# Selective-scan kernel: scan inputs of every second state from TensorE, y sums with h as the moving operand

## The chip, the cores and the metric

The kernel runs on one core of a Trainium2 chip. The metric is the device time of one execution in microseconds (us), taken as the median of several runs. TensorE (PE in the profile), VectorE (DVE), ScalarE (ACT), GpSimd (POOL) and SyncE (SP) each work through their own list of instructions in order and wait for one another through semaphores.

## The reference

The input x has 16 sequences of 256 steps and 256 features, with one conditioning vector each. Four layers follow one another: a low-rank adapter made from the conditioning vector (L0), a two-way selective state-space layer with a gated MLP (L1), a transformer block with 16 heads of 64 (L2) and one with 16 heads of 16 (L3). The part that the change touches is the state-space layer; for each sequence it is done once forwards and once backwards in time:

```python
xs, z = split(h @ in_w);  xs = silu(xs)                 # 512 inner channels each
proj = xs @ xproj_w
dt = softplus(proj[..., :512] + dt_bias)
Bm, Cm = proj[..., 512:576], proj[..., 576:640]         # 64 states
A = -exp(A_log)                                          # 512 x 64
def step(hst, ins):                                      # over the 256 time steps
    dA = exp(dt_t[:, :, None] * A)
    hst = hst * dA + (dt_t * x_t)[:, :, None] * B_t[:, None, :]
    y_t = einsum('bds,bs->bd', hst, C_t)
y = ys + xs * Dskip
return y * silu(z) @ out_w
```

Everything is in float32.

## The kernel before

**Units and states.** A unit is one sequence in one direction: 32 units, done one after the other. For each unit the kernel loops over the 64 states, so there are 2048 steps k = (u, s). In a step one state of all 512 channels is handled over all 256 times: 4 chunks (IC) of 128 channels on the partitions, each with 256 times along the free dimension, hence tiles h of 128 x 1024.

**One step.** `drive` (four steps ahead, AHEAD = 4) lets POOL write the scan's input h = dtx * B, where B of one state is a row that a DMA has spread over all partitions (`load_b`, tiles bb, four states a load) (L931). `decay` lets ACT write exp(dt * A) for the state into PSUM, in two tiles of 2 x 256 taken from a ring of three (L946, four instructions a state); column 0 of each chunk stays 0, so that a scan can run over two chunks and begin afresh at the second. `scan` lets DVE run two scans of 512 in place in h (L974); for the backward direction they run over the tile from its end. Then h is multiplied with C: in five of eight states by DVE with a C row that TensorE has spread into PSUM (`spread`, tile cs, L961, product L977), in three of eight by POOL with a C row that a DMA has spread (`load_c`, tile cb, product L981). `add_up` (two steps behind, BEHIND = 2) sums over the states in PSUM: eight transposes of 128 x 128 blocks of h add into y (L992), h being the stationary operand and the identity the moving one.

```python
nc.tensor.matmul(
    ys[u][:, t, c * P : (c + 1) * P], h[:, c, t * P : (t + 1) * P], ident, ...
    is_transpose=True, ...
```

**Beside the loop.** The loop over k is written out in Python; between its steps it advances two generators. `pend` does `back` of the unit before (the product with out_w) and `front` of the unit to come (projections pxz and pdt at L393 and L423, softplus, dt and dtx; load_front's weights). `other` does `rest(b)`, all of L1's MLP, L2 and L3 of a finished sequence (products dense, down, sc, pt, po, scT at L500 to L711), one or two pieces a step. After a unit's last state y is turned back (yt on ACT, py on TensorE, L1165 and L1172) and multiplied with silu(z). The scheduler may shift neighbouring instructions of an engine; POOL's products are kept in program order.

**Buffers.** h tiles come from a ring of NH = 11. PSUM has eight banks: two for y, three for the decays, one for cs, and two (ps_g) that all other products share. The last sequence's `rest` runs alone at the end and then also uses the decay and cs banks.

Of the kernel before, what the change touches and what calls it, by code (L numbers as in the profile page):

```python
# [15 lines left out]
P = 128  # L16
# [6 lines left out]
NS = 64  # L23
EPS = 1e-5


# [28 lines left out]
def kernel(ctx: ExitStack, tc: tile.TileContext, a: dict, out: bass.AP):  # L55
# [68 lines left out]
    SG = 4  # L124
    ND = 3
    NH = 11
    res = ctx.enter_context(tc.tile_pool(name="res", bufs=1))
# [6 lines left out]
    ps_y = ctx.enter_context(tc.tile_pool(name="ps_y", bufs=1, space=PSUM))  # L134
    ps_c = ctx.enter_context(tc.tile_pool(name="ps_c", bufs=1, space=PSUM))
    ps_g = ctx.enter_context(tc.tile_pool(name="ps_g", bufs=2, space=PSUM))
# [119 lines left out]
    for d in ("fwd", "bwd"):  # L256
        an = res.tile([P, IC, NS], F32, name=f"a_neg_{d}")
        nc.sync.dma_start(an, a[f"L1_cond_{d}_A_log"].rearrange("(c p) s -> p c s", p=P))
        nc.scalar.activation(an, an, AF.Exp)
        nc.vector.tensor_scalar(an, an, -1.0, None, ALU.mult)  # L260
        a_neg.append(an)
        w_bc.append(res.tile([P, IC, 2 * NS], F32, name=f"w_bc_{d}"))
        nc.sync.dma_start(w_bc[-1], chunked(a[f"L1_cond_{d}_xproj_w"])[:, :, DI:])
        w_out.append(res.tile([P, IC, D], F32, name=f"w_out_{d}"))
        nc.sync.dma_start(w_out[-1], chunked(a[f"L1_cond_{d}_out_w"]))


    decays = [ps_y.tile([P, 2, T], F32, name=f"decay{j}") for j in range(ND)]
    for dc in decays:
        nc.vector.memset(dc[:, :, 0:1], 0.0)  # L270

# [101 lines left out]
    def front(u):  # L373
# [15 lines left out]
        for m in range(0, 2 * IC, 2):  # L389
            px = halves(bank1("pxz"))  # L390
            for j in range(2):
                for c in range(DC):
                    nc.tensor.matmul(  # L393
                        px[:, j], w_in[:, c, (m + j) * P : (m + j + 1) * P], hT[:, c],
                        start=(c == 0), stop=(c == DC - 1),
                    )
                yield
            nc.scalar.copy(xz[:, m : m + 2], px)
        nc.scalar.activation(xz, xz, AF.Silu)
# [9 lines left out]
        yield  # L409
        pt = bank1("pct")  # L410
        for t in range(NT):
            nc.tensor.transpose(pt[:, t * P : (t + 1) * P], bc[:, t * P : (t + 1) * P], ident)
        cT = s2.tile([P, NT, NS], F32, name="cT")
        nc.scalar.copy(cT, pt[:, :T].rearrange("p (t s) -> p t s", t=NT)[:, :, NS:])
        yield


# [43 lines left out]
        tc.keep_in_program_order(nc.gpsimd.tensor_tensor(dtx, dt, xz[:, 0:IC], ALU.mult))  # L461
        st[u] = (xz, cT, bd, dt, dtx)
        yield

    def back(u, yg):
# [12 lines left out]
        for m in range(DC):  # L478
            xb = xs[b][:, m]
            nc.vector.scalar_tensor_tensor(  # L480
                xb, po[:, m], m_mamba[:, 4 + m, b : b + 1], xb, ALU.mult, ALU.add
            )
# [409 lines left out]

    bbs, cbs, ys, made, hs, skips = {}, {}, {}, {}, {}, {}
    cs = ps_c.tile([P, 2, T], F32, name="cs")
    steps = [(u, s) for u in range(len(units)) for s in range(NS)]
    turn = [0]

    def load_b(u, g):
        bd = st[u][2]
        bb = s3.tile([P, SG, T], F32, name="bb")  # L900
        nc.sync.dma_start(bb, bd[g * SG : (g + 1) * SG, :].partition_broadcast(P))
        bbs[u, g] = bb

    def load_c(u, g):
        bd = st[u][2]
        cb = s3.tile([P, 3, T], F32, name="cb")
        nc.sync.dma_start(
            cb,
            bd[NS + 8 * g + 1 : NS + 8 * g + 8 : 3, :].partition_broadcast(P),
        )  # L910
        cbs[u, g] = cb

    def drive(k):
        u, s = steps[k]
        if s % SG == 0:
            if s == 0:
                load_b(u, 0)
            if s + SG < NS:
                load_b(u, s // SG + 1)
            if s % 8 == 0:  # L920
                load_c(u, s // 8)
        if s == 0:
# [4 lines left out]
            skips[u] = skip  # L927
        h = s3.tile([P, IC, T], F32, name="h", bufs=NH)
        bb = bbs[u, s // SG][:, s % SG]
        tc.keep_in_program_order(  # L930
            nc.gpsimd.tensor_tensor(h, st[u][4], bb.unsqueeze(1).to_broadcast([P, IC, T]), ALU.mult)  # L931
        )
        hs[k] = h

    def decay(k):
        u, s = steps[k]
        d = units[u][1]

        when = slice(1, T) if d == 0 else slice(T - 2, None, -1)
        made[k] = []  # L940
        for i in range(2):
            dc = decays[turn[0] % ND]
            turn[0] += 1
            for j in range(2):
                c = 2 * i + (j if d == 0 else 1 - j)
                nc.scalar.activation(  # L946
                    dc[:, j, 1:T], st[u][3][:, c, when], AF.Exp, scale=a_neg[d][:, c, s : s + 1]
                )
            made[k].append(dc)


    near = [k for k, (u, s) in enumerate(steps) if s % 8 in (0, 2, 3, 5, 6)]
    nth = {k: i for i, k in enumerate(near)}

    def spread(i):

        if i >= len(near):
            return
        u, s = steps[near[i]]
        for t in range(NT):  # L960
            nc.tensor.transpose(  # L961
                cs[:, i % 2, t * P : (t + 1) * P], st[u][1][:, t, s : s + 1].to_broadcast([P, P]), ident
            )

    def scan(k):
        u, s = steps[k]
        d = units[u][1]
        h = hs[k]
        for i, dc in enumerate(made.pop(k)):
            hv = h[:, 2 * i : 2 * i + 2].rearrange("p c t -> p (c t)")  # L970
            dv = dc.rearrange("p c t -> p (c t)")
            if d == 1:
                hv = hv[:, ::-1]
            nc.vector.tensor_tensor_scan(hv, dv, hv, 0.0, ALU.mult, ALU.add)  # L974
        if k in nth:
            c = cs[:, nth[k] % 2]
            nc.vector.tensor_tensor(h, h, c.unsqueeze(1).to_broadcast([P, IC, T]), ALU.mult)  # L977
        else:
            c = cbs[u, s // 8][:, (s % 8) // 3]
            tc.keep_in_program_order(  # L980
                nc.gpsimd.tensor_tensor(h, h, c.unsqueeze(1).to_broadcast([P, IC, T]), ALU.mult)  # L981
            )

    def add_up(k):
        u, s = steps[k]
        if s == 0:
            ys[u] = ps_y.tile([P, NT, DI], F32, name="y")

        for n, h in enumerate(([skips.pop(u)] if s == 0 else []) + [hs.pop(k)]):
            for t in range(NT):  # L990
                for c in range(IC):
                    nc.tensor.matmul(  # L992
                        ys[u][:, t, c * P : (c + 1) * P], h[:, c, t * P : (t + 1) * P], ident,
                        start=(s == 0 and n == 0 and c == 0),
                        stop=(s == NS - 1 and c == IC - 1), is_transpose=True,
                        skip_group_check=True,
                    )

# [140 lines left out]
    for k in range(AHEAD):  # L1139
        drive(k)  # L1140
    decay(0)
    spread(0)
    spread(1)
    other = late()
    for k in range(len(steps) + BEHIND):
        if k < len(steps):
# [6 lines left out]
            if k + 1 < len(steps):  # L1153
                decay(k + 1)
        if k >= BEHIND:
            add_up(k - BEHIND)
        if k - 1 in nth:
            spread(nth[k - 1] + 2)
        if k >= BEHIND:
            u, s = steps[k - BEHIND]  # L1160
            if s == NS - 1:
                b, d = units[u]
                yt = s1.tile([P, NT, DI], F32, name="yt", tag="uu")
                for t in range(NT):
                    nc.scalar.copy(yt[:, t], ys[u][:, t])  # L1165
                yg = s1.tile([P, IC, T], F32, name="yg", tag="pr")
                for i in range(2):
                    py = halves(bank1("py"))
                    for j in range(2):
                        c = 2 * i + j  # L1170
                        for t in range(NT):
                            nc.tensor.transpose(py[:, j, t * P : (t + 1) * P], yt[:, t, c * P : (c + 1) * P], ident)  # L1172
                    nc.vector.tensor_tensor(
                        yg[:, 2 * i : 2 * i + 2], py, st[u][0][:, IC + 2 * i : IC + 2 * i + 2], ALU.mult
                    )
                pend = beside((u, yg), u + 2)
# [5 lines left out]
    drain(other)  # L1182
    alone += [None] + [t.rearrange("p c t -> p (c t)") for t in (decays[0], cs, decays[1])]
    alone += [None, decays[2].rearrange("p c t -> p (c t)")]
    while waiting:
# [29 lines left out]
```

## Time and profile before

| | |
|---|---|
| median of 3 runs | 7622.63 us (7620.03 to 7626.16) |
| span of the profiled execution, first to last instruction | 7616.3 us |
| median less span | 6.3 us |
| mean granted TensorE clock | 0.932 |
| first scan, last scan (start) | 139.5 us, 7383.1 us |
| DMA share of the 16 engines, q1 | 26.7%, 669.44 MB |
| sum of TensorE's waits on y for POOL's C product (L981) | 639.1 us |
| sum of ACT's waits on decay for DVE's scan | 1289.9 us |

The page gives no time of its own for the profiled execution beside its span; the median of the runs stands for what lies around it. In a group's line of the profile the columns are: line, engine, operation, out<-in by the program's names, shapes, how often (x), then busy time in us, mean ns of one, and the idle time of the engine just before the group with what ended most of it. PEld is the loading of TensorE's stationary operand. Matmul records overlap, so that their mean length is not their rate.

### The profile page before, as it was taken

The numbers are of one execution on the slowest core, as the hardware profiler recorded it, in microseconds if no ns is written. First come the engines' busy times: TensorE is split into PE (matmuls) and PEld (weight loads), VectorE is DVE, ScalarE is ACT, GpSimd is POOL, SyncE is SP. The second block draws the span as 40 slices with busy tenths as digits, with TensorE's granted clock in tenths as the row PEclk, the third lists the DMA queues.
The fourth block names the chain that finished last, engine by engine and source line by source line (L and its number), as shares of the span: only waits on it lengthen the run. The fifth ranks groups of instructions, "written<-read, shape, count | busy, mean of one in ns | idle before, by whom it ended". The sixth has DMA issues, their size and how long they took to land.

```text
span 7616.3 us, 100847 instructions
## 1 busy us (share of the span) xinstructions
PE 6249.2 (82%) x35471; PEld 4952.4 (65%) x35471; DVE 6860.6 (90%) x6887; ACT 5431.2 (71%) x12141; POOL 6843.8 (90%) x2959
## 2 busy tenths in 40 slices
PE   7568888888888888888888888888888888888778
PEld 4456676666667666676666666666666766666655
DVE  3988999999999999999999999999999999999982
ACT  4567777777777777777777777777777777777753
POOL 3999999999999999999999999999999999999960
PEclk8679999999999999999999999999999999999999
DMA  4112232222322222232222223222232222322221
GB/s 166 54 65 92 89 102 76 87 92 88 103 85 93 80 91 95 92 103 73 88 92 91 100 86 98 78 92 93 87 106 79 94 84 89 101 91 89 73 68 49
DMA packets 331644, 675.90 MB, mean 89 GB/s; under 512 B 24724, under 2 KB 204032, under 8 KB 326784
## 3 DMA queue, kind: packets, MB, share of 16 engines
q1 hardware_dynamic: 331136, 669.44, 26.7%
q8 instruction: 280, 4.59, 0.2%
q14 instruction: 228, 1.87, 0.1%
HBM read 650.22 MB, written 10.75 MB: 87 GB/s over the span
## 4 chain that ended last, share of the span: by engine, by line
DVE 47%; POOL 15%; issue 14%; ACT 12%; PE 10%; DVEq 0%; POOLq 0%; ACTq 0%
DVE h L974 34%; POOL h L931 8%; DVE h L977 8%; ACT decay L946 5%; POOL h L981 5%; PE y L992 3%; DVE maxima L682 1%; ACT L155 1%; PE dense L500 1%; PE down L511 1%; PE bank L108 1%; PE po L605 1%; POOL uu L452 1%; POOL dt L458 1%; POOL dtx L461 1%
## 5 line engine op out<-in xcount | busy, mean ns | idle before, releaser
L974 DVE TENSOR_TENSOR_SCAN h<-decay,h 128x512 f32<-128x512 f32 x4096 | 4748.8, 1213 | 283.1 <-ACT decay L946 196.6
L931 POOL TENSOR_TENSOR h<-dtx,bb 128x1024 f32<-128x1024 f32 x2048 | 4793.5, 2367 | 129.2 <-PE y L992 128.4
L992 PE MATMUL y<-ident,h 128*128 128x128 f32 x16384 | 2385.3, 292 | 693.0 <-POOL h L981 639.1
L992 PEld LDWEIGHTS y<-ident,h 128*128 128x128 f32 x16384 | 2054.6, 151 | 1047.6 <-POOL h L981 733.1
L946 ACT ACTIVATE decay<-dt,a_neg_bwd 128x255 f32<-128x255 f32 x4096 | 1816.8, 471 | 759.9 <-DVE h L974 718.3
L946 ACT ACTIVATE decay<-dt,a_neg_fwd 128x255 f32<-128x255 f32 x4096 | 1824.6, 474 | 613.0 <-DVE h L974 571.6
L981 POOL TENSOR_TENSOR h<-h,cb 128x1024 f32<-128x1024 f32 x768 | 1813.2, 2361 | 289.8 <-DVE h L974 275.1
L977 DVE TENSOR_TENSOR h<-h,cs 128x1024 f32<-128x1024 f32 x1280 | 1533.5, 1215 | 66.2 <-PE cs L961 56.6
L961 PE MATMUL cs<-ident,cT 128*128 128x128 f32 x2560 | 521.6, 294 | 131.8 <-DVE h L977 130.3
L961 PEld LDWEIGHTS cs<-ident,cT 128*128 128x128 f32 x2560 | 331.4, 147 | 216.0 <-DVE h L977 192.0
L572 PE MATMUL sc<-k,q 64*128 64x256 f32 x960 | 293.4, 429 | 16.7 <-ACT ex L581 16.0
L393 PE MATMUL pxz<-hTm,w_in 128*128 128x256 f32 x1024 | 267.6, 388 | 15.9 <-DVE maxima L682 12.1
L679 PE MATMUL sc<-kd,qk 128*128 128x512 f32 x490 | 251.4, 614 | 33.5 <-DVE maxima L682 20.8
L700 PE MATMUL scT<-qk,kd 128*128 128x256 f32 x984 | 251.1, 386 | 28.7 <-DVE qk L691 23.2
L581 ACT ACTIVATE ex<-sc,nmax 128x256 f32<-128x256 f32 x480 | 222.7, 468 | 71.2 <-DVE nmax L577 68.5
L423 PE MATMUL pdt<-xz,w_dt 128*128 128x256 f32 x1024 | 247.3, 385 | 0.0
L572 PEld LDWEIGHTS sc<-k,q 64*128 64x128 f32 x960 | 172.6, 200 | 105.3 <-issue 34.2
L393 PEld LDWEIGHTS pxz<-hTm,w_in 128*128 128x128 f32 x1024 | 181.4, 194 | 53.1 <-DVE maxima L682 15.5
L700 PEld LDWEIGHTS scT<-qk,kd 128*128 128x128 f32 x984 | 175.5, 190 | 60.7 <-ACT pr L429 25.0
L577 DVE TENSOR_REDUCE nmax<-sc 128x2 f32<-128x512 f32 x240 | 163.9, 683 | 49.5 <-PE sc L572 48.8
L423 PEld LDWEIGHTS pdt<-xz,w_dt 128*128 128x128 f32 x1024 | 190.7, 194 | 22.2
L595 ACT COPY exT<-pt 128x512 f32<-128x512 f32 x240 | 140.0, 583 | 86.2 <-PE pt L591 84.0
(350 smaller groups left out, 7571.4 us busy)
## 6 DMA issues: line engine op xcount, KB each, us to landing
bb<-bd SPq DMA_DIRECT2D x512, 512.0 KB
cb<-bd SPq DMA_DIRECT2D x256, 384.0 KB
l2w<-in_L_cond_W_dram SPq DMA_DIRECT2D x32, 1024.0 KB
l3w<-in_L_cond_W_dram SPq DMA_DIRECT2D x32, 1024.0 KB
l1w<-in_L_cond_mlp_w_dram SPq DMA_DIRECT2D x48, 512.0 KB
w_in<-in_L_cond_fwd_in_w_dram SPq DMA_DIRECT2D x16, 1024.0 KB
w_dt<-_L_cond_fwd_xproj_w_dram SPq DMA_DIRECT2D x16, 1024.0 KB
w_in<-in_L_cond_bwd_in_w_dram SPq DMA_DIRECT2D x16, 1024.0 KB
```

The lines of the kernel that those rows point to most:

```text
L393: nc.tensor.matmul(px[:, j], w_in[:, c, (m + j) * P : (m + j + 1) * P], hT[:, c], start=(c == 0), stop=(c == DC - 1),)
L423: nc.tensor.matmul(pp[:, j], w_dt[:, c, (m + j) * P : (m + j + 1) * P], xz[:, c], start=(c == 0), stop=(c == IC - 1),)
L572: nc.tensor.matmul(sc[:, t], q[base : base + 64, ch, t * P : (t + 1) * P], k[base : base + 64, ch], start=True, stop=True,)
L679: nc.tensor.matmul(sc, q[:, g, t * P : (t + 1) * P], kd[g % 2][:, 2 * i : 2 * i + 2], start=True, stop=True)
L700: nc.tensor.matmul(sc[:, kt], kd[g % 2][:, j, kt * P : (kt + 1) * P], q[:, g], start=True, stop=True)
L931: nc.gpsimd.tensor_tensor(h, st[u][4], bb.unsqueeze(1).to_broadcast([P, IC, T]), ALU.mult)
L946: nc.scalar.activation(dc[:, j, 1:T], st[u][3][:, c, when], AF.Exp, scale=a_neg[d][:, c, s : s + 1])
L961: nc.tensor.transpose(cs[:, i % 2, t * P : (t + 1) * P], st[u][1][:, t, s : s + 1].to_broadcast([P, P]), ident)
L974: nc.vector.tensor_tensor_scan(hv, dv, hv, 0.0, ALU.mult, ALU.add)
L977: nc.vector.tensor_tensor(h, h, c.unsqueeze(1).to_broadcast([P, IC, T]), ALU.mult)
L981: nc.gpsimd.tensor_tensor(h, h, c.unsqueeze(1).to_broadcast([P, IC, T]), ALU.mult)
L992: nc.tensor.matmul(ys[u][:, t, c * P : (c + 1) * P], h[:, c, t * P : (t + 1) * P], ident, start=(s == 0 and n == 0 and c == 0), stop=(s == ...
```

## The change

Every second state (odd s) gets its scan input from TensorE and its decays in SBUF; even states keep POOL's input and have their decays in PSUM.

- `diagonals`: for each group of four states POOL multiplies the identity with two columns of B, which gives diagonal matrices dg (128 x 512 an instruction); bT is B turned on TensorE in `front`, where C was turned before.
- `turn`: once a unit, dtx is transposed into xT (8 transposes, 2 ACT copies).
- `put_in`: for an odd state, 8 products xT x dg write the scan's input into PSUM, slot 1. One step later DVE scans it there.
- `decay`: an even state's decays go to PSUM slot 0, an odd state's into an h tile. Column 0 of dt is set to 1e34 (APART) and a_neg is kept at or below -1e-30 (LEAST), so that exp gives 0 there; one scan of 1024 then covers all four chunks.
- C: all rows by DMA (four states a load); even states are multiplied on POOL, odd ones on DVE.
- `add_up`: two products of 512 columns a state with the identity as the stationary and h as the moving operand, without transposing.
- Backward units have time turned round once, when xz is copied, and once when the result is added to x; scans always run forwards.
- y no longer has to be turned back (yt and py go). NH is 9. PSUM: y two banks, slots 0 and 1 two each, ps_g two.

```diff
-    ND = 3
-    NH = 11
+    NH = 9
...
-        nc.vector.tensor_scalar(an, an, -1.0, None, ALU.mult)
+        nc.vector.tensor_scalar(an, an, -1.0, LEAST, ALU.mult, ALU.min)
...
-    decays = [ps_y.tile([P, 2, T], F32, name=f"decay{j}") for j in range(ND)]
+    slots = [ps_y.tile([P, IC, T], F32, name=f"slot{j}") for j in range(2)]
...
-            nc.scalar.copy(xz[:, m : m + 2], px)
+            nc.scalar.copy(xz[:, m : m + 2], px[:, :, ::-1] if d else px)
...
+        tc.keep_in_program_order(nc.gpsimd.memset(dt[:, :, 0:1], APART))
...
+    def diagonals(u, g):
+        dg = s3.tile([P, NT, SG // 2, P], F32, name="dg")
+        tc.keep_in_program_order(
+            nc.gpsimd.tensor_tensor(
+                dg,
+                ident.unsqueeze(1).unsqueeze(1).to_broadcast([P, NT, SG // 2, P]),
+                st[u][4][:, :, g * SG + 1 : (g + 1) * SG : 2].unsqueeze(3).to_broadcast([P, NT, SG // 2, P]),
+                ALU.mult,
+            )
+        )
...
+    def turn(u):
+        xT = s1.tile([P, NT, DI], F32, name="xT")
+        for t in range(NT):
+            pt = bank1("pxt")
+            for c in range(IC):
+                nc.tensor.transpose(pt[:, c * P : (c + 1) * P], st[u][3][:, c, t * P : (t + 1) * P], ident)
+            nc.scalar.copy(xT[:, t], pt)
...
     def decay(k):
+        if s % 2:
+            dc = hs[k] = s3.tile([P, IC, T], F32, name="h", bufs=NH)
+        else:
+            dc = slots[0]
+        for c in range(IC):
+            nc.scalar.activation(dc[:, c], st[u][2][:, c], AF.Exp, scale=a_neg[d][:, c, s : s + 1])
+
+    def put_in(k):
+        u, s = steps[k]
+        dg = dgs[u, s // SG]
+        for t in range(NT):
+            for c in range(IC):
+                nc.tensor.matmul(
+                    slots[1][:, c, t * P : (t + 1) * P], xTs[u][:, t, c * P : (c + 1) * P],
+                    dg[:, t, s % SG // 2], start=True, stop=True,
+                )
...
     def scan(k):
+        h, ps = hs[k], slots[s % 2]
+        c = cbs[u, s // SG][:, s % SG].unsqueeze(1).to_broadcast([P, IC, T])
+        if s % 2:
+            nc.vector.tensor_tensor_scan(flat(ps), flat(h), flat(ps), 0.0, ALU.mult, ALU.add)
+            nc.vector.tensor_tensor(h, ps, c, ALU.mult)
+        else:
+            nc.vector.tensor_tensor_scan(flat(h), flat(ps), flat(h), 0.0, ALU.mult, ALU.add)
+            tc.keep_in_program_order(nc.gpsimd.tensor_tensor(h, h, c, ALU.mult))
...
     def add_up(k):
+            for i in range(0, IC, 2):
+                nc.tensor.matmul(
+                    ys[u][:, i : i + 2], ident, h[:, i : i + 2],
+                    start=(s == 0 and n == 0), stop=(s == NS - 1),
+                )
...
             if k + 1 < len(steps):
-                decay(k + 1)
+                if s % 2:
+                    decay(k + 1)
+                    decay(k + 2)
+                else:
+                    put_in(k + 1)
+            if s == NS - 1 and k + 1 < len(steps):
+                turn(u + 1)
         if k >= BEHIND:
             add_up(k - BEHIND)
-        if k - 1 in nth:
-            spread(nth[k - 1] + 2)
```

## The prediction

> **What bounds the kernel now.** I read the page's busy totals first, then the costliest groups, then windows, and last TensorE's timeline, because the change puts work there.
>
> ```profile
> span 7616.3 us, 100847 instructions
> PE 6249.2 (82%) x35471; PEld 4952.4 (65%) x35471; DVE 6860.6 (90%) x6887; ACT 5431.2 (71%) x12141; POOL 6843.8 (90%) x2959
> L974 DVE TENSOR_TENSOR_SCAN h<-decay,h 128x512 f32<-128x512 f32 x4096 | 4748.8, 1213 | 283.1 <-ACT decay L946 196.6
> L931 POOL TENSOR_TENSOR h<-dtx,bb 128x1024 f32<-128x1024 f32 x2048 | 4793.5, 2367 | 129.2 <-PE y L992 128.4
> L992 PE MATMUL y<-ident,h 128*128 128x128 f32 x16384 | 2385.3, 292 | 693.0 <-POOL h L981 639.1
> L981 POOL TENSOR_TENSOR h<-h,cb 128x1024 f32<-128x1024 f32 x768 | 1813.2, 2361 | 289.8 <-DVE h L974 275.1
> L977 DVE TENSOR_TENSOR h<-h,cs 128x1024 f32<-128x1024 f32 x1280 | 1533.5, 1215 | 66.2 <-PE cs L961 56.6
> L961 PE MATMUL cs<-ident,cT 128*128 128x128 f32 x2560 | 521.6, 294 | 131.8 <-DVE h L977 130.3
> L423 PE MATMUL pdt<-xz,w_dt 128*128 128x256 f32 x1024 | 247.3, 385 | 0.0
> ```
>
> DVE and POOL share the bound at 90%, taking turns; the loop over states runs from the first scan at 139.5 us to the last at 7383.1, or 3.54 us for each of 2048 states. TensorE is behind them, at 82% by its overlapping records. The last line matters most: the program calls that product 512 times and the profile has 1024, so a true f32 product is two instructions, while a transpose (y: 8 x 2048 = 16384) is one.
>
> Mean durations overlap, so TensorE's price is the distance between starts. Timeline of TensorE (start, length, group, count):
>
> ```profile
> 127.23 2.75 PE L215 MATMUL pmod<-silc,wmod 128*128 128x16 f32 x24
> ...
> 3068.38 1.04 PE L992 MATMUL y<-ident,h 128*128 128x128 f32 x8
> ...
> 3079.81 2.32 PE L511 MATMUL down<-q,l2out 128*128 128x256 f32 x10
> 3081.97 0.60 PE L961 MATMUL cs<-ident,cT 128*128 128x128 f32 x4
> ...
> 7442.38 1.88 PE L773 MATMUL pv<-wv,hT 128*128 128x512 f32 x4
> 7444.10 1.88 PE L773 MATMUL decay<-wv,hT 128*128 128x512 f32 x4
> ```
>
> Ten instructions of 256 columns take 2.16 us to the next group: 216 ns each. Four of 512 take 7444.10 - 7442.38 = 1.72: 429 ns. Eight transposes of 128 take (1.04 - 0.27) / 7 = 109 ns, 0.27 being the shortest record of one. So every f32 instruction streams at 0.84 ns a column, and a full product, being two, costs 1.68. Where a load of new weights is all there is (pmod, 16 columns), one comes every (2.75 - 0.26) / 23, about 108 ns.
>
> **The change, part by part.** All on TensorE's clock as those rows show it.
>
> *Sums of y.* Removed: 16640 transposes (skips included) x 109 = 1814 us. Added: 2080 tiles x 2 products of 512 columns x 2 instructions = 8320 x 429 = 3570 us. The moving operand is read twice, and that is a loss of 1756 us.
>
> *Scan inputs of odd states (put_in).* Added: 1024 x 8 products of 128 columns, each with its own weights, 16384 instructions. No row shows a full product of this size. Lower bound: streaming and loading overlap as in y, 109 ns (1.79 ms). Upper: they follow one another, 218 ns (3.57 ms). I take 109, because y's rows load 128x128 weights for 128 columns at just that pace.
>
> *C.* The 2560 spread transposes go: 2560 x 109 = 279 us. py's 256 go and turn's 256 come: even; likewise the ACT copies yt and xT.
>
> TensorE thus gains 3570 + 1792 - 1814 - 279 = +3.27 ms of work, against 1367 us in which it is idle now. That decides the case. Every remaining product, counted in the changed kernel's instruction order and priced at 109, 215 or 429 ns (the attention sums po, whose weights are 32 or 64 columns wide, counted at 0.35 and 0.8, since many of their starts nearly coincide), gives 3.33 ms. TensorE's total is 3570 + 1792 + 3331 = 8.69 ms; 64 us of it stand before the first put_in, 174 in the tail, **8455 us in the loop**.
>
> *The other engines per pair of states.* DVE: from 4 scans of 512 and 1.25 products (6.4 us) to 2 scans of 1024 and one product. A 1024 scan lies between 1.21 (all fixed cost) and 2.43 us (twice); with some 150 ns fixed, as 512 and 1024 columns of a product (683 and 1215 ns) suggest, I take 2.28: 5.8 us with L977's 1.22. Its source and target in PSUM are new to it; even 2.43 changes nothing here. POOL: from 2 drives and 0.75 C products (6.5 us) to one drive, one C product and half a diagonal (128x512, between 0.29, the 128-column select, and 2.37; I take half of 2.37): 5.3 us. ACT: eight decays as before, 3.7 us. TensorE needs 8455 / 1024 = 8.26 us on average. So savings of 0.6 us on DVE and 1.2 on POOL are real and lie under TensorE: worth nothing.
>
> Where the rest of the network has nothing to do, a pair has only 5.2 us of TensorE work and DVE's 5.8 decides; by the instruction order 86 pairs are such, 43 us in all.
>
> *Waits.* put_in waits for DVE's product of the odd state before it (one PSUM slot), and behind it on TensorE stand both y sums, the next unit's front and the rest of the network; DVE's odd scan waits for it. Cover: between two put_ins the order has 3.43 us of y sums and on average 3.0 of other products, against scan plus product, 3.5 us. Without the y sums there it would cost up to 3.5 us a pair. y of an even state waits for POOL's C product, released a whole pair earlier. In today's loop TensorE idles 430 us before groups other than y, cs and py, on ACT and DVE; now nothing absorbs that. I keep 430; bounds 0 and 1287 (with y's, cs's and py's 857).
>
> *SP and DMA.* Issues of B and C go from 768 to 1024, bytes from 369 to 403 MB, 5% on a DMA share of 27%; each is issued four states ahead (some 17 us at the new pace). Nothing. The memset of dt, the floor under a_neg, the reversed copies and NH are free beside TensorE: at most 32 x 0.31 us on POOL.
>
> *Sum.* 139.5 before the loop + 8455 + 43 + 430 + 232 tail = 9300 us of span. The median of the runs, 7622.6, lies 6 us over today's span: **9306, say 9300 us**.
>
> **Two rules beside the rows.** The clock first. Windows (us, then busy PE, PEld, DVE, ACT, POOL, granted clock):
>
> ```profile
> 200.00:600.00 400.00, 235.48 (x1234) 208.09 (x1233) 359.73 (x326) 236.80 (x511) 388.81 (x169) 0.73 0.18 58
> 1000.00:2000.00 1000.00, 837.99 (x4802) 669.42 (x4802) 934.58 (x936) 741.01 (x1655) 940.81 (x406) 0.94 0.28 91
> 7200.00:7300.00 100.00, 81.94 (x472) 59.80 (x471) 98.71 (x106) 64.23 (x140) 92.48 (x40) 1.00 0.24 85
> ```
>
> The clock is lowest where TensorE idles most, and my spacings are those at full clock. If 0.94 stays, the loop is 8455 / 0.94 = 8995 and the time 9850. The Trainium skill, "TensorE: Matmul & The Clock Gate", Part 1, says that throttling is the default and sustained activity releases it. By it a denser TensorE gets 1.0, which is the sum above.
>
> For the y sums, the rows give a full product twice a transpose's price per column. The same page (Terms) has transpose mode 4x faster for FP32. By that, y would cost four times its transposes, about 7.3 ms, and the kernel 13 ms; no row here supports more than twice, so the row stands.
>
> **Rivals.** (1) *Put_in is dearer.* Loads and streams of different weights do not overlap in full products (218 ns): +1.79 ms, 11.1 ms; or the scan and product of the odd state stand open before each put_in, up to 1024 x 3.5 = +3.6 ms, 12.9 ms. Against: y's pace with as many loads, and the order just described. 9%. (2) *Faster: TensorE is not the bound.* If these f32 products ran as one instruction each, y would cost 1785 and put_in 893 us, TensorE's loop 5.8 ms, and DVE decides: 1024 x 5.8 = 5.9 ms + 0.5 ms of its other work + 378 outside = 6.8 ms. It decides from the point where y and put_in cost 3.67 ms together instead of 5.36 (then 8455 - 1690 + 43 + 430 + 378 is today's time). Against: every f32 group that is no transpose has twice its program's count. 5%. (3) *The two cancel*, products a third cheaper than their rows: 1%.
>
> **How the numbers follow.** The forecast, TensorE as the bound, has 85%. Its floor without any stall is 8.87 ms; its upper end with the 0.94 clock 9.85, with all idle kept 10.1. The range 8850 to 9950 leaves out rival 1, rival 2 and the forecast's far end, together under 2 in 10. About 0.2% is what a measurement of this kernel can tell from no change: faster 5%, within 1%, slower 94%.
>
> **What would show it.** Right: TensorE near 95% busy in every slice with the clock near 1.0; y x8320 at 429 ns between starts and put_in x16384 near 109; DVE about 70%, POOL about 60%, both idle mostly on TensorE's put_in and y; the chain of waits mostly on PE. Wrong: half those counts, DVE still at 90%, put_in spaced at 200 ns or more, or long TensorE waits for DVE before put_in.

## Result, and the profile after

The changed kernel takes 10257.8 us (10256.2 to 10259.7, four runs) against 7624.4 for the kernel before: a ratio of 1.345, with a 95% interval of 1.343 to 1.347. The forecast was 9300 in a range of 8850 to 9950. The sign was right; the time lies 958 us above the forecast and outside the range.

From the page of the changed kernel: totals, then slices, then the groups that the change touches. Columns as before: busy time and mean ns of one, then the idle time in front and what ended most of it.

```profile
span 10255.5 us, 109898 instructions
PE 9288.4 (91%) x40975; PEld 6134.5 (60%) x40975; DVE 6677.8 (65%) x4548; ACT 5506.1 (54%) x12141; POOL 5593.9 (55%) x2735
...
PE   7889898998989999899998989989899898998998
...
PEclk8999999999999999999999999999999999999998
...
L992 PE MATMUL y<-h,ident 128*128 128x512 f32 x8192 | 3839.0, 597 | 1.0 <-POOL h L983 1.0
L945 POOL TENSOR_TENSOR h<-dtx,bb 128x1024 f32<-128x1024 f32 x1024 | 2412.4, 2356 | 1781.1 <-issue 1487.3
L982 DVE TENSOR_TENSOR_SCAN h<-slot,h 128x1024 f32<-128x1024 f32 x1024 | 2343.2, 2288 | 1523.7 <-POOL h L945 1384.4
L979 DVE TENSOR_TENSOR_SCAN slot<-h,slot 128x1024 f32<-128x1024 f32 x1024 | 2342.3, 2287 | 939.9 <-PE slot L966 939.9
...
L966 PE MATMUL slot<-dg,xT 128*128 128x128 f32 x16384 | 2139.0, 285 | 222.1 <-DVE h L980 220.6
...
L903 POOL TENSOR_TENSOR dg<-ident,bT 128x512 f32<-128x512 f32 x512 | 533.6, 1042 | 2478.4 <-PE slot L966 2478.4
```

DVE and POOL, at 90% before, have fallen to 65 and 55% (70 and 60 were forecast), and TensorE is the busiest engine. But it isn't the near-solid 95% that the prediction named as its sign: slices of 8 stand among the 9s. And the idle columns of POOL and DVE hold thousands of microseconds: POOL's diagonals (L903) wait for TensorE's put_in, DVE's even scan (L982) waits for POOL's drive.

To see what this costs TensorE, I count its instructions between the first and the last scan at their full-speed spacing (109, 215 or 429 ns, as in the prediction) and call the rest of the loop the stall; it holds waits, stretches at a lower clock, and whatever real spacing exceeds these three figures.

| | span | loop | TensorE's work in it | stall |
|---|---|---|---|---|
| before | 7616.3 | 7243.6 | 5185.0 | 2058.6 |
| after | 10255.5 | 9865.2 | 8458.2 | 1407.0 |
| forecast | 9300 | 8928 | 8455 | 473 |

The counted work is what the prediction had, within 4 us. The stall is three times the 473 us (430 + 43) of the sum, and that is 934 of the 958 us missed; of the rest 19 lie outside the loop (390 us for 372). Of the 1407, TensorE sat idle for 868: 475 until DVE, 387 until ACT and 6 until others let it go on.

### The profile page after: what moved, and what is told of

It reads as the page before. It is cut to its first block, busy times and chain, and to the rows that moved or that the text cites. A ratio compares the mean times of both kernels' runs of the same rounds, so it can differ in the third digit from the quotient of the medians.

```text
span 10255.5 us, 109898 instructions
## 1 busy us (share of the span) xinstructions
PE 9288.4 (91%) x40975; PEld 6134.5 (60%) x40975; DVE 6677.8 (65%) x4548; ACT 5506.1 (54%) x12141; POOL 5593.9 (55%) x2735
## 5 line engine op out<-in xcount | busy, mean ns | idle before, releaser
L992 PE MATMUL y<-h,ident 128*128 128x512 f32 x8192 | 3839.0, 597 | 1.0 <-POOL h L983 1.0
L945 POOL TENSOR_TENSOR h<-dtx,bb 128x1024 f32<-128x1024 f32 x1024 | 2412.4, 2356 | 1781.1 <-issue 1487.3
L982 DVE TENSOR_TENSOR_SCAN h<-slot,h 128x1024 f32<-128x1024 f32 x1024 | 2343.2, 2288 | 1523.7 <-POOL h L945 1384.4
L979 DVE TENSOR_TENSOR_SCAN slot<-h,slot 128x1024 f32<-128x1024 f32 x1024 | 2342.3, 2287 | 939.9 <-PE slot L966 939.9
L966 PEld LDWEIGHTS slot<-dg,xT 128*128 128x128 f32 x16384 | 2069.9, 200 | 494.8 <-DVE h L980 305.7
L966 PE MATMUL slot<-dg,xT 128*128 128x128 f32 x16384 | 2139.0, 285 | 222.1 <-DVE h L980 220.6
L992 PEld LDWEIGHTS y<-h,ident 128*128 128x128 f32 x8192 | 1473.0, 192 | 1228.0 <-issue 1194.9
L959 ACT ACTIVATE slot<-dt,a_neg_bwd 128x256 f32<-128x256 f32 x2048 | 973.6, 475 | 1970.8 <-DVE h L982 1926.5
L903 POOL TENSOR_TENSOR dg<-ident,bT 128x512 f32<-128x512 f32 x512 | 533.6, 1042 | 2478.4 <-PE slot L966 2478.4
L959 ACT ACTIVATE slot<-dt,a_neg_fwd 128x256 f32<-128x256 f32 x2048 | 973.9, 476 | 1065.3 <-DVE h L982 1015.1
L980 DVE TENSOR_TENSOR h<-slot,cb 128x1024 f32<-128x1024 f32 x1024 | 1253.6, 1224 | 34.5
```

The source lines that it names most:

```text
L903: nc.gpsimd.tensor_tensor(dg, ident.unsqueeze(1).unsqueeze(1).to_broadcast([P, NT, SG // 2, P]), st[u][4][:, :, g * SG + 1 : (g + 1) * SG ...
L945: nc.gpsimd.tensor_tensor(h, st[u][3], bb.unsqueeze(1).to_broadcast([P, IC, T]), ALU.mult)
L959: nc.scalar.activation(dc[:, c], st[u][2][:, c], AF.Exp, scale=a_neg[d][:, c, s : s + 1])
L966: nc.tensor.matmul(slots[1][:, c, t * P : (t + 1) * P], xTs[u][:, t, c * P : (c + 1) * P], dg[:, t, s % SG // 2], start=True, stop=True,)
L979: nc.vector.tensor_tensor_scan(flat(ps), flat(h), flat(ps), 0.0, ALU.mult, ALU.add)
L980: nc.vector.tensor_tensor(h, ps, c, ALU.mult)
```

## Where the stall comes from

The view of waits of the changed kernel (engine, line, waited for: total us, times, longest):

```profile
ACT slot L959 <- DVE h L982: 2941.6, 865, 12.1
POOL dg L903 <- PE slot L966: 2478.4, 494, 13.9
POOL h L945 <- issue: 1487.3, 352, 11.3
DVE h L982 <- POOL h L945: 1384.4, 755, 5.4
...
DVE slot L979 <- PE slot L966: 939.9, 415, 8.7
...
PE slot L966 <- DVE h L980: 220.6, 146, 4.9
```

TensorE's own wait at put_in for DVE, the one that the prediction weighed (rival 1), is small: 221 us. The large waits stand on the other engines and form a ring. The timeline of one pair shows it (start, length, engine, group; in brackets the idle time in front and who ended it), TensorE's lines first, then DVE's, ACT's and POOL's:

```profile
3540.26 1.95 PE L966 MATMUL slot<-dg,xT 128*128 128x128 f32 x16
3542.05 1.88 PE L992 MATMUL y<-h,ident 128*128 128x512 f32 x4
3543.77 1.03 PE L391 MATMUL pxz<-hTm,w_in 128*128 128x256 f32 x4
...
3551.41 1.12 PE L677 MATMUL sc<-kd,qk 128*128 128x512 f32 x2 [2.32 <-ACT v L842]
3554.10 2.07 PE L677 MATMUL sc<-kd,qk 128*128 128x512 f32 x2 [1.57 <-ACT xz L396]
3555.97 3.59 PE L966 MATMUL slot<-dg,xT 128*128 128x128 f32 x16
3559.38 1.89 PE L992 MATMUL y<-h,ident 128*128 128x512 f32 x4
...
3547.98 2.29 DVE L982 TENSOR_TENSOR_SCAN h<-slot,h 128x1024 f32<-128x1024 f32 x1 [2.18 <-POOL h L945]
...
3550.36 0.48 ACT L959 ACTIVATE slot<-dt,a_neg_bwd 128x256 f32<-128x256 f32 x1 [9.31 <-DVE h L982]
3550.78 0.58 ACT L842 COPY v<-pv 128x512 f32<-128x512 f32 x1
...
3553.48 0.56 ACT L396 COPY xz<-pxz 128x512 f32<-128x512 f32 x1
...
3542.29 1.04 POOL L903 TENSOR_TENSOR dg<-ident,bT 128x512 f32<-128x512 f32 x1 [10.26 <-PE slot L966]
3543.30 2.35 POOL L983 TENSOR_TENSOR h<-h,cb 128x1024 f32<-128x1024 f32 x1
3545.60 2.34 POOL L945 TENSOR_TENSOR h<-dtx,bb 128x1024 f32<-128x1024 f32 x1
...
3561.41 2.35 POOL L945 TENSOR_TENSOR h<-dtx,bb 128x1024 f32<-128x1024 f32 x1 [11.15 <-issue]
```

Read from the first line: put_in ends about 3542.2 and frees the older of two dg buffers. POOL has stood 10.26 us at the diagonal; it now does diagonal, C product and drive in a row, 5.7 us. DVE's even scan starts 0.04 us after the drive. ACT's decays of the next even state need the slot that this scan has read, so ACT has stood 9.31 us, with the copy of v and then that of xz queued behind the decays. TensorE waits for both copies, 2.32 and 1.57 us, before it comes to the next put_in, which frees the next dg buffer. That put_in then takes 3.59 us instead of 1.95 for the same 16 instructions: by the clock records TensorE had half its clock from 3552.57 to 3559.39. In all, 540 us of the loop ran at half clock, which cost at most half of that, 270.

Why does DVE want the drive at that very moment? In the instruction order, the scheduler has put each even scan three pairs (six states) ahead of the odd scan that it is written beside, in 1014 of 1024 pairs; as written, the lead is none. `drive` is only four states ahead in the written loop. So POOL's lead is used up: at 1016 of the 1024 even scans POOL had not begun any drive beyond the one that is scanned, and the scan starts 0.04 us (median) after that drive ends. Its result is consumed as it is made, and whatever holds POOL up reaches DVE, ACT and, over DVE's results and ACT's copies, TensorE. One such thing is a dg buffer. The other is in all likelihood an h tile: for 1487 us of POOL's waits at the drive (352 times) the profile names nothing ("issue"), but each of these 352 drives starts within 0.25 us after a y sum ends, as the one at 3561.41 does; by chance about one in fifteen would.

The theory: the excess stall comes from this order, with the dg buffers as the first link. The rivals: put_in or the f32 products cost more than their spacing (the prediction's rival 1), the ring of h tiles is simply too small for POOL (NH 9), or TensorE's y sums are in the way.

## Experiments

Ratios are to the kernel before on the same chip, with a 95% interval. The last columns are TensorE's work and stall in the loop and the granted clock.

| run | us | ratio | work | stall | clock |
|---|---|---|---|---|---|
| after | 10257.8 | 1.345 (1.343–1.347) | 8458 | 1407 | 0.968 |
| e1 scans in written order | 9393.3 | 1.233 (1.229–1.236) | 8458 | 545 | 0.994 |
| e2 eight h tiles | 9709.6 | 1.274 (1.271–1.278) | 8458 | 860 | 0.988 |
| e3 y by transposes | 9584.7 | 1.258 (1.254–1.262) | 6740 | 2452 | 0.937 |
| e4 put_in twice | 11709.8 | 1.537 (1.532–1.541) | 10251 | 1070 | 0.977 |
| e5 = e1 + e3 | 8465.7 | 1.110 (1.107–1.113) | 6741 | 1339 | 0.982 |
| e6 three dg buffers | 9793.7 | 1.284 (1.281–1.288) | 8458 | 939 | 0.985 |
| e7 before, h moving | 8838.8 | 1.159 (1.156–1.162) | 6880 | 1561 | 0.962 |
| e8 put_in for a quarter | 9105.0 | 1.194 (1.190–1.197) | 5845 | 2861 | 0.908 |
| e9 e8, product from PSUM | 8716.8 | 1.143 (1.141–1.145) | 5845 | 2483 | 0.919 |
| e10 no put_in | 8743.2 | 1.146 (1.145–1.148) | 4905 | 3441 | 0.878 |
| e11 e10, free order | 8478.6 | 1.112 (1.111–1.114) | 4904 | 3176 | 0.874 |

**e1: DVE's scans in the written order.**

```diff
-            nc.vector.tensor_tensor_scan(flat(ps), flat(h), flat(ps), 0.0, ALU.mult, ALU.add)
-            nc.vector.tensor_tensor(h, ps, c, ALU.mult)
+            tc.keep_in_program_order(
+                nc.vector.tensor_tensor_scan(flat(ps), flat(h), flat(ps), 0.0, ALU.mult, ALU.add)
+            )
+            tc.keep_in_program_order(nc.vector.tensor_tensor(h, ps, c, ALU.mult))
...
-            nc.vector.tensor_tensor_scan(flat(h), flat(ps), flat(h), 0.0, ALU.mult, ALU.add)
+            tc.keep_in_program_order(
+                nc.vector.tensor_tensor_scan(flat(h), flat(ps), flat(h), 0.0, ALU.mult, ALU.add)
+            )
```

> The only change: DVE's scans and the odd state's C product are kept in the order in which the program writes them, so that an even scan is directly followed by the odd scan of its pair (in the changed kernel's instruction order it is followed by the odd scan six states behind it, and h tiles of four finished even states wait for their y sums). Theory H (h tiles run out: POOL's drive waits for TensorE's y to release a tile, DVE's even scan waits for POOL, the odd scan and ACT's copies queue behind it, and TensorE waits for those): the wait of DVE's even scan for POOL's drive falls from 1384 us to below 300, ACT's wait for it from 2940 to below 1500, TensorE's stalls by 700 to 1000 us, time 9250 to 9600 us. Rival R (TensorE's excess over its counted work comes from the rest of the network's own chains, handovers and the clock, whatever DVE's order): 10100 to 10300 us.

9393.3 us, as theory H expected: 864 less, all of it stall (1407 to 545), with the same TensorE instructions. The edit moves more than DVE's list: the scheduler rearranged ACT's too (three quarters of it by ten places or more), TensorE's hardly (under 1%) and POOL's practically not. So what is shown is the effect of the order as a whole. Totals and clock slices of e1's page:

```profile
PE 9012.2 (96%) x40975; PEld 5947.4 (63%) x40975; DVE 6625.7 (71%) x4548; ACT 5455.5 (58%) x12141; POOL 5599.6 (60%) x2735
...
PEclk8999999999999999999999999999999999999998
```

and its view of waits:

```profile
POOL h L987 <- DVE h L985: 3290.8, 815, 12.2
ACT slot L959 <- DVE h L985: 2306.6, 961, 8.9
...
PE slot L966 <- DVE h L982: 181.3, 242, 5.7
```

POOL no longer waits for dg (86 us) or for an h tile to any amount; it waits for DVE, as an engine with time to spare should. Its lead is back: at 907 of the even scans two further drives have begun. ACT still waits 2307 us at the slot, where below 1500 had been expected, but TensorE's idle time that ends with ACT falls from 387 to 61 us: wait totals of engines that have slack say nothing by themselves. TensorE's idle time falls from 868 to 278 us, and the time at half clock from 540 to 14. The forecast, 9300, is 1.0% below this kernel: in the written order the changed kernel takes 1.23 times the time before, and the order that the scheduler gave it adds the rest.

**e2: a smaller ring of h tiles** (`NH = 9` to `NH = 8`).

> The only change: the ring of h tiles has 8 instead of 9. Theory H: one tile fewer while the even scans still run six states ahead (in 855 of 1024 pairs, four ahead in 163): POOL's drive waits longer for y, TensorE's stalls grow, time 10350 to 10900 us. Rival R: no change, 10200 to 10300 us.

9709.6, 548 us faster with less room, against both expectations: the ring's size is not a plain shortage. But the edit isn't clean, since the scheduler answered it: the lead of six states shrinks to four in 163 pairs, and ACT's and TensorE's orders change as well (POOL's doesn't). POOL's wait at the diagonals falls to 1012 us, while DVE's wait for the drive even grows to 1842. Which of these brought the gain is left open; it agrees with e1 only in that the order, and not the work, is what moved.

**e3: y by transposes again, in the changed kernel.**

```diff
-            for i in range(0, IC, 2):
-                nc.tensor.matmul(
-                    ys[u][:, i : i + 2], ident, h[:, i : i + 2], ...
+            for t in range(NT):
+                for c in range(IC):
+                    nc.tensor.matmul(
+                        ys[u][:, t, c * P : (c + 1) * P], h[:, c, t * P : (t + 1) * P], ident, ...
+                        is_transpose=True, ...
```

> The y sums alone are undone: eight transposes a state with h as the stationary operand, y turned back at a unit's end (yt, py). TensorE's counted work falls by 1756 us (8320 x 429 against 16640 x 109) less 28 for py. Theory H and the prediction's term: TensorE stays the bound or near it; time falls by 1400 to 1800 us, to 8450 to 8850 us. Rival P (TensorE's work is not what sets the time; the chain put_in, odd scan, product and the h ring does): falls by less than 700 us, to above 9550 us.

TensorE loses 1718 us of work, the time only 673, which is rival P's side: in this order TensorE's work alone does not set the time. The stall grows from 1407 to 2452: with the same ring of waits and shorter y sums, put_in comes due sooner and waits longer. View of waits of e3:

```profile
POOL dg L903 <- PE slot L966: 2731.6, 504, 13.1
...
PE slot L966 <- DVE h L980: 656.1, 395, 6.9
```

**e4: put_in written twice** (`for t in list(range(NT)) * 2`, the second pass over the first).

> put_in is issued twice for every odd state (the second time over the first, the same values), 16384 more instructions. If TensorE is the bound and put_in costs its 109 ns an instruction: +1790 us, to 11900 to 12200 us, a little less if it fills stalls. If loads and streams of a full product with its own weights do not overlap (218 ns): +3.5 ms, 13.7 ms. If a chain with slack on TensorE set the time: under +900 us.

1452 us more, for 16384 more instructions; the time lies somewhat under the 11900 to 12200 expected. At 109 ns they are 1792 us of work, of which 337 come out of stall. At 218 ns they would have been 3.57 ms. So a 128-column f32 product with new weights each time streams at nearly the pace of a transpose, and rival 1's first half is refuted.

**e5: written order and y by transposes** (e1 and e3 together).

> DVE's scans and odd products in written order (as in e1_scan_order) and the y sums as transposes again (as in e3_y_transposed). If the y term of the prediction is right in size and only DVE's order hid it in e3: 1500 to 1800 us under e1, that is 7600 to 7900 us. If TensorE's work in y does not set the time even in the written order: above 8700 us.

928 us below e1 for 1718 us of work, between the two expectations (7600 to 7900, above 8700). TensorE is at 89%; view of waits:

```profile
POOL h L987 <- DVE h L985: 2214.4, 710, 9.9
...
PE slot L966 <- DVE h L982: 328.6, 485, 2.5
PE y L997 <- POOL h L987: 287.7, 228, 3.8
```

TensorE's two waits on the recurrence (put_in for DVE, y for POOL's C product) now are 616 us (some 190 in e1); the y sums used to cover them. So the new form of y costs 928 us here, but its 1718 us are not all to be had back. Even so this is 11% over the kernel before.

**e6: three dg buffers** (`bufs=3` for dg, paid for with one bb buffer). DVE's order stays that of the changed kernel.

> The changed kernel with three instead of two buffers for the diagonals dg (and two instead of three for bb, to make room); DVE's list is as in the changed kernel, even scans six states ahead. Theory H1 (it is the wait of POOL's dg for TensorE's put_in that delays the drive and with it DVE and ACT): POOL's wait of 2478 us on put_in falls below 800, time 9400 to 9800 us. Theory H2 (it is the ring of h tiles: drive waits for y): POOL waits for y instead, time within 10100 to 10300 us.

464 us faster, the stall down by 468 to 939. View of waits:

```profile
POOL h L945 <- issue: 1727.5, 364, 8.9
POOL h L945 <- PE y L992: 1712.6, 447, 11.1
...
DVE h L982 <- POOL h L945: 753.4, 787, 4.8
```

The wait at dg has gone from POOL's list; POOL now waits at the drive for TensorE's y to give back an h tile (the 364 waits put down to "issue" end just after a y sum too), and DVE's wait for the drive is nearly halved. So the dg buffers are about half of the 862 us that e1 takes out, shown with the order held: TensorE's, DVE's and POOL's lists are the same, ACT's all but. The other half goes with the written order; that it is the h ring is likely by these lines but was not isolated (e2).

**e7: the new y alone, in the kernel before** (two products of 512 in `add_up`, no yt and py).

> The kernel before with one part of the change alone: y summed with h as the moving operand in f32 products of 512 columns, and no yt and py. TensorE's counted work in the loop goes from 5.2 to 6.9 ms. Theory T (an f32 product column costs twice a transposed one, and TensorE becomes the third engine at the bound): slower, 7750 to 8400 us. If the products were no dearer than the transposes: 7500 to 7620 us, a little faster, because spread, yt and py waits shrink.

8838.8, beyond what was expected: 1212 us more for 1695 us more work on an engine that was at 82%. TensorE now is at 87% and POOL waits for it:

```profile
POOL h L931 <- PE y L991: 1561.7, 696, 8.6
...
DVE h L974 <- POOL h L931: 1249.2, 667, 6.9
```

Longer y sums hold h tiles longer, which holds POOL's drives and then DVE. Here an engine with spare time on average still gives its work's length to those who wait for a buffer from it.

**e8: less TensorE work.** y by transposes, written order, put_in for every fourth state only; the others by POOL, with their decays in the two slots in turn, made two states ahead.

```diff
-        if s % 2 == 0:
+        if s % 4 != 1:
             h = s3.tile([P, IC, T], F32, name="h", bufs=NH)
...
+            if s % 2:
+                tc.keep_in_program_order(nc.vector.tensor_tensor(h, h, c, ALU.mult))
...
+            if s % 4 == 0:
+                put_in(k + 1)
```

> A version meant to use what the runs so far show: y sums as transposes, DVE's scans in written order, one scan of 1024 a state and C by DMA as in the change, but put_in only for one state in four (s % 4 == 1); the other inputs by POOL, C on POOL for even states. Per four states POOL has 3 drives, 2 C products and a 128x256 diagonal, 12.3 us, DVE 4 scans and 2 products, 11.6 us, TensorE 1.8 us of put_in. Theory: POOL and DVE bind, TensorE has 6.1 ms of work: 6900 to 7400 us. Rival (put_in's chain with the scan before and after it stalls DVE wherever it stands): above 7620 us.

9105.0, a clear miss, on the rival's side (above 7620). One price was wrong. DVE's groups in e8:

```profile
L988 DVE TENSOR_TENSOR h<-h,cb 128x1024 f32<-128x1024 f32 x512 | 1110.1, 2168 | 14.9
L982 DVE TENSOR_TENSOR h<-slot,cb 128x1024 f32<-128x1024 f32 x512 | 625.3, 1221 | 16.0
```

The same product takes 1221 ns when one operand comes from PSUM and 2168 on average when all operands are in SBUF (from 1224 to 3482).

**e9: e8 with that product reading PSUM** (the states s % 4 == 3 scan into their slot; `nc.vector.tensor_tensor(h, ps, c, ...)`).

> Leaves nothing of the result out. As e8 (TensorE makes the scan input of every fourth state only, y by transposes, scans and products in the written order), with one edit: the states s%4 == 3 scan into their PSUM slot, so that DVE's product reads PSUM instead of two SBUF operands. Theory C (in e8 the product from SBUF shared something with POOL and took 2168 ns instead of 1221): the product falls back to some 1220 ns, the 512 of them give back about 485 us on DVE, and by the sum per four states (DVE 4 x 2.29 + 2 x 1.22 = 11.6 us, POOL 3 x 2.36 + 2 x 2.36 + 0.55 = 12.4 us) POOL is the bound at 3.1 us a state; with today's overhead of some 0.3 us a state 7400 to 8200. Rival W (the waits of e8 come from the written order itself, not from the long product): the product falls to 1220 but the time stays over 8700. Rival S (the place of the operand is not what made it long): the product stays at 2.2 us.

The groups of e9, POOL's C product and DVE's product of those states:

```profile
L992 POOL TENSOR_TENSOR h<-h,cb 128x1024 f32<-128x1024 f32 x1024 | 2411.6, 2355 | 1792.8 <-DVE h L990 1678.7 <-PE px L339 78.5 <-PE y L1002 26.6
...
L987 DVE TENSOR_TENSOR h<-slot,cb 128x1024 f32<-128x1024 f32 x512 | 625.7, 1222 | 12.8
```

The product is back at 1222 ns and the time 388 us lower; rival S is out. But at 8716.8 it is outside theory C's 7400 to 8200 and just inside rival W's side (over 8700): the rest is waits, POOL's for DVE above all, with no engine over 81%. Whether they come from the written order, as W has it, was not tried with this kernel.

**e10 and e11: no put_in.** All drives on POOL and y by transposes, as before the change; kept of it are one scan of 1024 a state, decays in two whole slots, C by DMA, reversed copies. DVE multiplies in five states of eight, reading PSUM. e10 in the written order, e11 with the order left to the scheduler (e11's form is shown).

```diff
+        dc = slots[s % 2]
...
+        if s % 8 in (0, 2, 3, 5, 6):
+            nc.vector.tensor_tensor_scan(flat(ps), flat(ps), flat(h), 0.0, ALU.mult, ALU.add)
             nc.vector.tensor_tensor(h, ps, c, ALU.mult)
```

> Leaves nothing of the result out. TensorE makes no scan input at all and sums y by transposes as in the kernel before; kept of the change: one scan of 1024 a state, decays for all four chunks in a slot of four, C by DMA, reversed copies. DVE takes the products of the states s%8 in (0, 2, 3, 5, 6) as before and scans those into their PSUM slot; POOL makes every drive and the other products; scans and products in the written order. Theory C (the loss of the change lies in TensorE's new work and the waits around it): without it POOL bounds at 1.375 x 2.36 = 3.25 us a state and DVE needs 2.29 + 0.625 x 1.22 = 3.05; the loop is 6.65 ms plus stalls, the time between 7100 and 7650, so at least as fast as before. Rival D (decays in two slots are too few: the slot is free only when the product of two states before has read it, and 1.86 us of ACT then stand before the next scan): long waits of DVE for ACT's slot, 8000 or more.

> Leaves nothing of the result out. As e10, with DVE's scans and products placed by the scheduler instead of in the written order. If the scheduler's placing is bad only where a drive or a slot is scarce (theory C), it runs DVE ahead here as in the changed kernel and the time lies 100 to 1500 above e10, with DVE waiting for POOL's drive. Rival: with no scan input from TensorE the even and the odd scans wait for the same kind of drive, the scheduler has no reason to draw them apart, and the time is within 100 of e10.

8743.2 and 8478.6. e10's view of waits:

```profile
PE y L992 <- POOL h L982: 1267.8, 560, 9.0
ACT slot L954 <- DVE h L977: 1244.2, 825, 6.9
POOL h L982 <- DVE h L980: 1200.7, 474, 11.1
...
DVE slot L975 <- ACT slot L954: 503.8, 315, 6.3
```

Theory C is refuted in its strong form: without any put_in the time still is 15% above that of before, although no engine has noticeably more to do than it had (DVE 6887 us busy for 6861, POOL 6839 for 6844, ACT 5579 for 5431, TensorE's work 4905 for 5185). Rival D is borne out in direction: two decay slots, each busy until its scan or product has read it, make ACT and DVE wait for each other (all of DVE's waits for ACT come to 974 us, 308 before); the kernel before had three half-size tiles in turn. DVE's waits for TensorE are up too, 785 us for 347, with less TensorE work. TensorE's timeline in e10 shows one reason:

```profile
4018.54 1.09 PE L992 MATMUL y<-ident,h 128*128 128x128 f32 x8 [1.49 <-DVE h L977]
4023.16 1.97 PE L992 MATMUL y<-ident,h 128*128 128x128 f32 x8 [3.52 <-POOL h L982]
```

The same eight transposes take 1.09 us, and 1.97 after a wait of 3.52: the clock records give full clock to the first and, from 4020.45 to 4027.27, half to the second. In e10 2031 us of the loop ran at half clock, 944 in the kernel before. How the loss divides between slots and clock wasn't tried. e11 is 265 us faster than e10, against both expectations: the written order isn't the better one in itself; in e1 it left POOL's lead intact, which is the likely reason why it helped there. No variant run here beats the kernel before.

## Why the prediction was right and wrong

*TensorE becomes the bound:* right in part. e4 adds work to TensorE alone and the time follows by 81%; in e1 TensorE is 96% busy. But 1718 us less work gave only 673 us in e3 and 928 in e5, because waits took its place.

*Sums of y, +1756 us of work:* the size is right (8320 instructions; four of 512 columns a state, 1.72 us from 3542.05 to the next group in the timeline above, against 0.87 for eight transposes at 109 ns). The rule of the Trainium skill that the prediction weighed, that transpose mode is four times as fast for FP32 ("TensorE: Matmul & The Clock Gate", Terms), isn't borne out here: the measured factor is two, for transposes of 128 columns that each load new weights.

*put_in, 109 or 218 ns:* 109 was nearly right; the 16 instructions at 3540.26 take 1.79 us to the next group, 112 ns each, and e4 doubles them.

*The other engines' prices:* scan of 1024, 2.28 taken and 2.288 measured, with an operand in PSUM; diagonal 1.18 taken, 1.04 measured; product 1.22. SP and DMA: nothing, as said; q1 moves 703 MB for 669, the 34 more that were worked out.

*The clock:* the sum took full clock; the changed kernel has 0.968 over its span. The Trainium skill's rule (the same page, Part 1: sustained activity releases the throttle) agrees in the main: the clock falls with TensorE's busy share, 0.994 at 96% (e1), 0.968 at 91% (after), 0.932 at 82% (before), 0.878 at 74% (e10), though e5 has 0.982 at 89%. The time at half clock goes with the stall, since e1 has nearly none of it; whether it is only an effect was not tried apart, and a stretch at half clock also lengthens the put_in that POOL waits for.

*Waits, 430 us (with 43 for idle pairs):* this is the step that failed. It took today's stall of groups other than y, cs and py and stopped at TensorE. What it said of TensorE's own waits held: put_in's was nearly covered (221 us), and y's wait for POOL's C product, "released a whole pair earlier", came to 1.0 us. It didn't ask whether POOL's drive still comes before the scan that needs it, listed POOL's new diagonals as 1.2 us of work without asking what they wait for and what stands behind them in POOL's kept order (a C product and a drive), and called the smaller ring of h tiles free beside TensorE without a reason. In the order that ran, with even scans six states ahead, the drive is consumed at once; POOL's diagonals wait 2478 us for put_in, its drive 1487 us (most likely for h tiles), DVE's even scan 1384 us for the drive, and ACT's single list closes a ring back to TensorE. The term measured 1407 us. The order is 862 of the 934 us by which it was missed (e1); with the order held, a third dg buffer alone takes out 468 (e6). The upper bound for the term, 1287, was made of today's waits, which could not contain a wait that didn't exist yet.

That the sum comes within 1% of e1 is luck in part. Its stall of 545 us is 278 us of idle time, of which put_in's wait, 185, was put at nothing, and only 72 stand before the kinds of group that the 430 were for; the clock costs at most 7 us, and the remaining 260 are spacings wider than the three prices (put_in's median is 112 ns for 109), another term that the sum didn't have. In the changed kernel the same split is 868 us idle (222 at put_in, 1 at y, 645 elsewhere), at most 270 by the clock, and again some 270 of spacing.

*Rivals:* (1) put_in dearer: refuted by e4 in its first half (218 ns). Of its second half, up to 3.6 ms for DVE's scan and product open before each put_in, 221 us are there as TensorE's wait. (2) and (3), a cheaper f32 product: refuted by the counts and spacing.

## What to carry to other kernels

Moving work to the engine with spare time is priced by that engine's own rows: an f32 product costs two instructions where a transpose costs one. Then follow every new instruction in the order that the scheduler gives: what it waits for, what is queued behind it, and how much lead is left between the producer and the consumer. A lead written in the loop was worth nothing here once the scheduler let the consumer run ahead by more.

Buffers that are handed from engine to engine (dg, h, decay slots) should be counted in that order too; e6's one more dg buffer gave 464 us, and with e10's two whole slots for three half tiles DVE's waits for ACT rose from 308 to 974 us.

## What had not been expected of the hardware

A DVE product of 128x1024 with all operands in SBUF took 2168 ns on average and up to 3482 beside POOL's products, and 1221 with one operand in PSUM (e8, e9). It is POOL that makes the difference: the 30 of the 512 that ran while POOL was idle took 1225 ns on average, while the product with an operand in PSUM stayed at 1221 beside POOL's work too. POOL suffered as well: its drive took 2594 ns on average in e8 and 2362 in e9. In the kernel before, DVE's product reads C from PSUM, and so it never showed. What it is that the two engines share was not shown; that the place of one operand decides was.
